# Two Fourier layers: written order on every engine, later statistics, scaling on GpSimd, and a second layer that takes x from the scaled images

## The chip, the cores and the metric

The kernel runs on one core of a Trainium2 chip. The metric is device time in microseconds of one execution. A core has TensorE (PE, with PEld for its weight loads), VectorE (DVE), ScalarE (ACT), GpSimd (POOL), and SyncE (SP), which here only issues DMAs. All data are 32-bit floats.

## The reference

The input is x of shape (2, 56, 128, 128): two images with 56 channels. Two layers of the same form are applied, each `x = x + block(groupnorm(x))`. The group norm takes groups of four of the last axis's 128 positions, over all of an image's channels and rows. Cut to what matters, the block is:

```python
def spectral_conv(x, w, b):                      # 16 + 16 by 16 modes are kept
    xf = jnp.fft.rfft2(x, norm='forward')
    top = jnp.einsum('bihw,iohw->bohw', xf[:, :, :M1, :M2], _c(w[0]))
    bot = jnp.einsum('bihw,iohw->bohw', xf[:, :, -M1:, :M2], _c(w[1]))
    ...
    return jnp.fft.irfft2(of, s=(H, W), norm='forward') + b[None, :, None, None]

xa = x.reshape(B * K, 1, H, W)                   # B = 2 images, K = 56 channels
xn = inorm(xa, g1, b1)
k, q, v = (fno_layer(xn, ...) for each)          # spectral_conv + 1x1 skip, 8 heads
scores = jnp.einsum('baks,bals->bakl', qh, kh) * scale
out = jnp.einsum('bakl,bals->baks', jax.nn.softmax(scores, axis=-1), vh)
out = fno_layer(out, Pw, Pb, Psw, Psb)
att = inorm(out + xa, gan, ban)
an = inorm(att, g2, b2)
h = fno_layer(an, M0w, ..., norm=True, act=True)  # act is the exact gelu
h = fno_layer(h, M1w, ..., norm=True, act=False)
y = inorm(h, gmo, bmo) + att
```

## The kernel before

An image lies in SBUF in `X2` with the channels on partitions, twice: rows of two kinds of eight on partitions 0 to 55 and 64 to 119. Two more partitions (56 and 120) hold a row of scales. Nearly all of the block is done on the 32 x 16 kept modes, in tiles of 448 columns; full images are touched only for the transform, for the gelu and for the end. A full image is handled in eight pieces ("units") of 1024 columns, numbered n = 2A + v.

For each layer L and image b the work is a set of Python generators. Each emits instructions and yields a number, its cost in microseconds as the author sees it:

- `turn` / `turned` transpose eight rows on PE (L361 in layer 0, L363 in layer 1), copy them on ACT (L366, L369) into the tile `P[b]` and take `bn_stats` on DVE (L371). `modes_chain` makes mean and scale from them (L459 to L468), scales the plane (L477 on ACT, L479 on DVE), transforms along one axis (L483), transposes on DVE (L488), and transforms along the other (L384).
- `gram` (L511), `gram_chain`, `scores` (L597, L578), `values` (L620), `softmax_chain`, `mix_chain`, `heads` (L691) and `norms_chain` do attention and the norms by way of small matrices. `scale_x` multiplies the whole image by the scales of its groups, in place, in eight DVE instructions of 120 x 1024 (L550), and then writes the scale rows with two DMAs.
- `gelu`: synthesis of each unit (L753), a matmul with the scaled image (`mixed`, L768), Gelu on ACT (L835), `bn_stats` on DVE (L837), transposing back (`turn_back`, L817, L818) and a transform (`forward`, L805, and a DVE copy, L810).
- `h_chain`: transposes on DVE (L851), small matrices, a chain of small DVE and ACT steps, the diagonals `dg` (L432), their spread by a matmul (L437), and `inverse` (L399, L404).
- `end`: synthesis (L753), `mixed` (L768), a sum on DVE (L943) and the residual x. In layer 0, and for image 0 of layer 1, POOL adds x from the ring `xr` of three buffers (L946), loaded from DRAM. Layer 0 writes image 0 to the DRAM tile `store` for this. For image 1 of layer 1, x is made again from the scaled image: `unscale` multiplies it on DVE, in place, by the inverse scales (L775), and `add_x` adds it by a matmul (L782). Layer 0 then calls `turned` for the next layer.
- `prepare` and `relay` make weight matrices of a layer (some 95 small POOL instructions; then PE L316, DVE L320, PE L327, ACT L331), and `build` / `build_m` expand them on POOL (L337, L345).

`_woven(lead, *bulks)` runs a lead chain and, after each of its yields, as many pieces of the bulks as their costs fill. `_with` steps a second generator once per piece. The Python order is thus one written order. It is not the order in which the engines run: the framework's scheduler orders the instructions of each engine by dependences and its own costs when the program ends. In `build`, `build_m` and `scale_x`, `tc.keep_in_program_order` binds single instructions.

PSUM is handed out as two `bank` tiles (2 KB per partition) and three `pair` tiles (4 KB). SBUF tiles with one name share one place, so that a new use waits for the readers of the old one.

## Time and profile before

| what | value |
|---|---|
| median of 3 runs | 551.45 us (550.92 to 551.50) |
| profiled execution | 547.76 us, span 546.0 us |
| PE busy | 458.8 us, 84% of the span |
| DVE busy | 318.6 us, 58% |
| ACT busy | 190.3 us, 35% |
| POOL busy | 158.5 us, 29% |
| HBM read, written | 21.02 MB, 11.01 MB |
| mean granted PE clock | 0.919 |

The span is the time from the first to the last recorded instruction, and the profiled execution is a single run with 1.76 us around that span. A line such as L768 names a line of the kernel printed above. In a group, "out<-in" are tile names, then the shape of output and input, then the busy time in us, the mean duration in ns, and the idle time just before with what ended it. In a stretch the columns are its length, then busy time and count of each engine, the granted PE clock, the share of the DMA engines that was busy, and GB/s.

### The profile page before, as it was taken

What the parts mean: (1) busy time and instruction counts of PE and PEld (TensorE: products, weight loads), DVE (VectorE), ACT (ScalarE), POOL (GpSimd) and SP (SyncE); (2) the same over time, 40 slices, a digit from 0 to 9 for tenths busy, and PEclk for the clock granted to TensorE, in tenths of its full rate; (3) what the DMA queues carried; (4) which work ended last, traced back from release to release, by engine and by line L of the source; (5) the groups of instructions that cost most, each with busy time, mean ns of one, the idle gap of its engine ahead of it and who ended that gap; (6) DMA issues with size and microseconds to landing.
All of it is one profiled execution on the core that took longest, in us unless ns stands there. A gap on an engine that the chain in (4) does not pass through costs nothing.

```text
span 546.0 us, 14842 instructions
## 1 busy us (share of the span) xinstructions
PE 458.8 (84%) x6696; PEld 315.0 (58%) x6696; DVE 318.6 (58%) x556; ACT 190.3 (35%) x242; POOL 158.5 (29%) x205
## 2 busy tenths in 40 slices
PE   2467999898699999989587799989599999986695
PEld 2325869686485566636443468778376556544431
DVE  1465352926735784777578562717715775766585
ACT  2443330524435436614223240344237356502000
POOL 2297509950000000044539924000000000055300
PEclk9998898989797998989679999999797998988698
DMA  8994001030100000016553320000000000027444
GB/s 181 232 196 73 4 2 46 4 89 2 20 2 2 1 2 1 1 35 212 175 136 100 98 78 6 3 4 4 2 3 1 1 2 1 1 56 236 149 129 141
DMA packets 13167, 33.24 MB, mean 61 GB/s; under 512 B 2080, under 2 KB 2848, under 8 KB 13088
## 3 DMA queue, kind: packets, MB, share of 16 engines
q1 hardware_dynamic: 12960, 32.23, 22.8%
q8 instruction: 52, 0.85, 0.7%
q10 hardware_dynamic: 144, 0.07, 0.1%
q14 instruction: 11, 0.09, 0.1%
HBM read 21.02 MB, written 11.01 MB: 59 GB/s over the span
## 4 chain that ended last, share of the span: by engine, by line
PE 53%; DVE 20%; POOL 7%; DMA 7%; ACT 6%; issue 5%; SPq 1%; DVEq 0%; POOLq 0%; ACTq 0%
PE pair L768 8%; PE pair L753 6%; PE pair L817 5%; POOL X L946 5%; PE pair L597 5%; PE bank L511 5%; PE bank L691 3%; DMA X<-x 3%; PE bank L805 3%; DMA xr<-x 3%; DVE WT L404 2%; DVE X L550 2%; PE bank L578 2%; PE bank L442 2%; PE bank L327 2%
## 5 line engine op out<-in xcount | busy, mean ns | idle before, releaser
L371 DVE BATCH_NORM_STATS2 stats<-P 128x6 f32<-128x448 f32 x64 | 36.1, 614 | 48.2 <-ACT P L366 32.3
L837 DVE BATCH_NORM_STATS2 stats<-P 128x6 f32<-128x512 f32 x64 | 40.7, 678 | 20.3 <-ACT P L835 20.3
L943 DVE SCALAR_TENSOR_TENSOR P<-P,hs,pair 128x1024 f32<-128x1024 f32 x32 | 40.1, 1270 | 12.7 <-PE pair L768 12.5
L835 ACT ACTIVATE P<-pair 128x1024 f32<-128x1024 f32 x32 | 32.6, 1025 | 32.4 <-PE pair L768 31.8
L946 POOL TENSOR_TENSOR X<-P,xr 128x1024 f32<-128x1024 f32 x16 | 37.5, 2355 | 19.4 <-DMA xr<-x 11.2
L393 POOL MEMSET WT<- 128x256 f32 x4 | 1.3, 313 | 139.4 <-PE bank L805 92.9
L817 PEld LDWEIGHTS pair<-C,P 120*128 120x128 f32 x256 | 29.0, 152 | 21.2 <-issue 8.5
L550 DVE TENSOR_TENSOR X<-X,gvr 120x1024 f32<-120x1024 f32 x32 | 40.3, 1303 | 0.0
L768 PE MATMUL pair<-X,Bs 57*64 57x512 f32 x256 | 40.2, 671 | 0.0
L768 PE MATMUL pair<-X,Be 57*64 57x512 f32 x256 | 38.6, 705 | 0.0
L817 PE MATMUL pair<-C,P 120*128 120x120 f32 x256 | 36.8, 291 | 0.5 <-DVE P L404 0.5
L511 PE MATMUL bank<-P 128*64 128x56 f32 (+1 forms) x1024 | 37.2, 238 | 0.0
L511 PEld LDWEIGHTS bank<-P 128*64 128x64 f32 (+1 forms) x1024 | 35.5, 152 | 2.1 <-issue 1.5
L597 PEld LDWEIGHTS pair<-xf,WU 64*64 64x64 f32 x1024 | 32.8, 135 | 5.3 <-issue 4.5
L597 PE MATMUL pair<-xf,WU 64*64 64x56 f32 x1024 | 35.9, 221 | 0.0
L818 ACT COPY WT<-pair 128x896 f32<-128x896 f32 x32 | 28.9, 906 | 14.0 <-PE pair L817 12.5
L753 PE MATMUL pair<-C,WT 32*128 32x128 f32 x512 | 24.1, 294 | 9.1 <-DVE WT L404 4.4
L753 PEld LDWEIGHTS pair<-C,WT 32*128 32x128 f32 x512 | 19.4, 189 | 20.5 <-issue 12.0
L369 ACT COPY P<-pair 128x896 f32<-128x896 f32 x16 | 14.5, 907 | 46.3 <-PE pair L363 46.3
L361 PE MATMUL pair<-C,X 56*128 56x56 f32 x256 | 16.7, 282 | 16.4 <-DMA X<-x 10.7
L363 PE MATMUL pair<-C,X 120*128 120x120 f32 x128 | 18.8, 297 | 13.4 <-POOL X L946 13.4
L363 PEld LDWEIGHTS pair<-C,X 120*128 120x128 f32 x128 | 14.9, 155 | 23.3 <-POOL X L946 20.0
(235 smaller groups left out, 850.0 us busy)
## 6 DMA issues: line engine op xcount, KB each, us to landing
X<-x SPq DMA_DIRECT2D x16, 448.0 KB
xr<-x SPq DMA_DIRECT2D x32, 224.0 KB
out<-P SPq DMA_DIRECT2D x32, 224.0 KB
store<-X SPq DMA_DIRECT2D x16, 224.0 KB
xr<-store SPq DMA_DIRECT2D x16, 224.0 KB
stage<-weights SPq DMA_DIRECT2D x2, 544.0 KB
C<-const_all SPq DMA_DIRECT2D x1, 621.0 KB
X<-x SPq DMA_DIRECT2D x2, 256.0 KB
```

The source lines that it names most:

```text
L363: T.transpose(p[:, s, N * e : N * e + 120], X2[:120, b, i, :], ident[:120, :120])
L371: V.bn_stats(stats[:, 2 * g + s, :], dst[:, 448 * s : 448 * s + 448])
L511: T.matmul(p[u : u + m, :K], lhsT=P[b][:, K * i : K * i + m], rhs=plane[b][:, i, :], start=(i < 2), stop=(i == N - 1), tile_position=(0, u ...
L550: tc.keep_in_program_order(V.tensor_tensor(v, v, _bc(st["gvr"][:120], 1, 8), ALU.mult))
L597: T.matmul(p[64 * e : 64 * e + 64, k, K * a : K * a + K], lhsT=WUv[64 * e : 64 * e + 64, t + k, a, :], rhs=xv[64 * e : 64 * e + 64, t + k, ...
L753: T.matmul(both[j // 2][:, j % 2, N * e : N * e + N], lhsT=Z[32 * j : 32 * j + 32, o : o + N], rhs=C["gw"][32 * j : 32 * j + 32, :], start ...
L768: T.matmul(p[64 * c : 64 * c + 64, r, :], lhsT=Bs[q, :], rhs=X2[q, b, s : s + 4, :].rearrange("p e w -> p (e w)"), start=False, stop=stop, ...
L817: T.transpose(p[:, r, N * e : N * e + 120], h3[:120, o : o + N], ident[:120, :120])
L835: S.activation(h3, both[v].rearrange("p r m -> p (r m)"), AF.Gelu)
L837: V.bn_stats(stats[:, 4 * A + 2 * v + r, :], h3[:, 512 * r : 512 * r + 512])
L943: V.scalar_tensor_tensor(h3, h3, st["hs"], both[v].rearrange("p r m -> p (r m)"), ALU.mult, ALU.add)
L946: G.tensor_tensor(dst, h3, xr[:, n % 3, :], ALU.add)
```

## The change

- **Order.** After the whole program is traced, `_in_order` adds a dependence, without a wait, from each instruction to the one before it on the same engine, for DVE, ACT, POOL, PE and SP. The engines' order is then the written one. The single `keep_in_program_order` calls go.
- **One unit late.** `turned` returns its statistics as a function, which `turn` and `end` call after the next piece; `gelu` defers the statistics and the copy of `forward` to after the next Gelu; `end` defers the sum (and what follows it) of a unit to after the matmuls of the next one.
- **Fillers.** `_woven` gets `spare`, a generator from which pieces are taken only if the bulks have run out. `scores` of image 1 and `gelu` of image 0 become such fillers, and the calls are rearranged. `scale_x` stands as a block behind the scores of its image. `prepare(1)` stands behind that of image 1. Relay of layer 1's weights moves to the end of image 0.
- **Scaling on POOL.** `scale_x` and `unscale` use POOL instead of DVE. `unscale` writes to the ring `xr` instead of in place.
- **x of the second layer.** Both images of layer 1 use `unscale` and `add_x`. The DRAM tile `store`, its 16 writes and its 16 reads go, and so does the POOL addition there.
- **Smaller edits.** In `modes_chain` the four scalings are written ahead, and transforms and transposes go by two in a pair (two DVE transposes of 896 columns for four of 448). `t` in `norms_chain` and `h_chain` moves from a bank to a pair. `mix_chain` and `heads` share one pair. The yielded costs are changed.

Core of the diff (renamings of queues and most changed costs are left out):

```diff
+def _in_order(tc, engines):
+    last = {}
+    for i in list(tc.nc.cur_bb.bb.instructions):
+        if i.engine in engines:
+            if i.engine in last:
+                info = mybir.DependencyInfo(mybir.DependencyClass.NoSync, mybir.DependencyReason.DATA)
+                tc.add_manual_dep(i, last[i.engine], info, reason="in order")
+            last[i.engine] = i.name
...
-def _woven(lead, *bulks):
+def _woven(lead, *bulks, spare=()):
...
             if cost is None:
+                cost = next(spare, None) if spare else None
+            if cost is None:
                 break
...
     def turn(b, stats):
+        before = None
         for g in range(8):
-            turned(b, g, 0, stats)
-            yield 0.9
+            count = turned(b, g, 0, stats)
+            if before:
+                before()
+            before = count
+            yield 1.1
+        before()
...
+        for j in range(0, 4, 2):
+            p = pair()
+            for k in range(2):
...
+                yield 0.6
+            V.transpose(
+                midv[:, :, 14 * j : 14 * j + 28].rearrange("p m (k i) -> p k i m", k=2),
+                p[:, :, :448].rearrange("p k (h i) -> p k i h", h=32),
+            )
...
     def scale_x(b, st):
         for s in range(0, 64, 8):
             v = X2[:120, b, s : s + 8, :]
-            tc.keep_in_program_order(V.tensor_tensor(v, v, _bc(st["gvr"][:120], 1, 8), ALU.mult))
+            (G.tensor_tensor(v, v, _bc(st["gvr"][:120], 1, 8), ALU.mult))
...
     def mix_chain(L, b, st):
+        st["pair"] = pair()
...
-        t = bank()[:, :448]
+        t = pair()[:, 0, :448]
...
     def unscale(b, A, v, by):
...
-        V.tensor_tensor(x8, x8, _bc(_bc(by[:120], 1, 4), 1, 2), ALU.mult)
+        to = xr[:120, (2 * A + v) % 3, :].rearrange("p (c s w) -> p c s w", c=2, s=4)
+        (G.tensor_tensor(to, x8, _bc(_bc(by[:120], 1, 4), 1, 2), ALU.mult))
...
                     S.activation(h3, both[v].rearrange("p r m -> p (r m)"), AF.Gelu)
-                    for r in range(2):
-                        V.bn_stats(stats[:, 4 * A + 2 * v + r, :], h3[:, 512 * r : 512 * r + 512])
-                    yield 0.9
+                    settle()
+                    after.append(lambda n=2 * A + v, h3=h3: count(n, h3))
+                    yield 1.1
...
+        def total(n, p):
+            h3 = P[b][:, 1024 * n : 1024 * n + 1024]
+            V.scalar_tensor_tensor(h3, h3, st["hs"], p.rearrange("p r m -> p (r m)"), ALU.mult, ALU.add)
+            if L == 0:
+                G.tensor_tensor(X2[:, b, 8 * n : 8 * n + 8, :].rearrange("p e w -> p (e w)"), h3, xr[:, n % 3, :], ALU.add)
+            else:
+                for c in range(2):
+                    Q.dma_start(
+                        out=far[b, c, :, n // 2, 2 * (n % 2) : 2 * (n % 2) + 2],
+                        in_=h3[64 * c : 64 * c + K].rearrange("p (r m) -> p r m", r=2),
+                    )
+            if L == 0:
+                ready(n + 2)
...
+        for A in range(4):
+            if before:
+                before()
+                before = None
             both = [pair(), pair()]
             synthesis(A, both, st["Z"])
             yield 1.0
             for v in range(2):
                 n = 2 * A + v
+                mixed(L, b, A, v, both[v], st["Be"], L == 0)
+                if L == 1:
+                    add_x(n, both[v])
+                    ready(n + 2)
+                if before:
+                    before()
+                before = lambda n=n, p=both[v]: total(n, p)
+                yield 2.1 if L == 1 else 1.1
+                if L == 0 and n > 2:
+                    counts.append(turned(b, n - 3, 1, stats))
+                    if len(counts) > 1:
+                        counts.pop(0)()
+                    yield 1.0
...
+        ux1, g0 = scores(L, 1, s1), gelu(L, 0, s0)
+        _run(_woven(gram_chain(L, 1, s1), scores(L, 0, s0)))
+        _run(scale_x(0, s0))
+        _run(_woven(softmax_chain(L, 0, s0), values(L, 0, s0), spare=ux1))
+        _run(_woven(mix_chain(L, 0, s0), heads(L, 0, s0), spare=ux1))
+        _run(_woven(norms_chain(L, 0, s0), ux1, values(L, 1, s1)))
+        _run(scale_x(1, s1))
         if L == 0:
             par, d, cpt, tcs = prepare(1)
             prs[1] = par, d
+        _run(_woven(softmax_chain(L, 1, s1), spare=g0))
+        _run(_woven(mix_chain(L, 1, s1), heads(L, 1, s1), spare=g0))
+        _run(_woven(norms_chain(L, 1, s1), g0))
         _run(_woven(h_chain(L, 0, s0), gelu(L, 1, s1)))
         stats = [new_stats(b) for b in range(B)] if L == 0 else [None, None]
+        more = relay(cpt, tcs, stage[:, :1024], [(0, 16), (16, 16), (32, 4)]) if L == 0 else iter(())
+        _run(_woven(h_chain(L, 1, s1), _with(end(L, 0, s0, stats[0]), more)))
...
+    _in_order(tc, [e.engine for e in (V, S, G, T, Q)])
```

In `ready(n)`, layer 0 loads unit n of x from DRAM into `xr`, and layer 1 calls `unscale` for it; two units are readied ahead of the loop.

## The prediction

> **What bounds the kernel now.** First the page: busy shares, then the slices.
>
> ```profile
> PE 458.8 (84%) x6696; PEld 315.0 (58%) x6696; DVE 318.6 (58%) x556; ACT 190.3 (35%) x242; POOL 158.5 (29%) x205
> PE   2467999898699999989587799989599999986695
> POOL 2297509950000000044539924000000000055300
> PEclk9998898989797998989679999999797998988698
> ```
>
> TensorE (PE) is the only engine near full. It has holes at the start and around slices 10, 19-23 and 36-38, and its clock drops beside most of them. POOL rests for long stretches. Second the stretches, cut where the work changes: columns are length, busy PE, PEld, DVE, ACT, POOL, clock, DMA.
>
> ```profile
> 0.00:51.90 51.90, 26.65 (x285) 17.79 (x285) 22.71 (x48) 18.87 (x22) 27.78 (x84) 1.00 0.83 179
> 51.90:94.60 42.70, 41.41 (x886) 35.91 (x885) 17.24 (x33) 10.34 (x17) 22.59 (x17) 0.88 0.06 17
> 94.60:158.40 63.80, 53.70 (x950) 44.25 (x948) 36.07 (x64) 23.18 (x31) 23.00 (x46) 0.92 0.12 25
> 158.40:233.70 75.30, 72.79 (x834) 46.00 (x832) 51.31 (x107) 40.53 (x49) 0.33 (x2) 0.93 0.01 2
> 233.70:275.80 42.10, 35.10 (x356) 22.37 (x358) 27.36 (x48) 11.04 (x16) 20.23 (x12) 0.81 0.51 153
> 275.80:316.80 41.00, 30.94 (x364) 16.26 (x364) 28.14 (x37) 12.31 (x14) 33.58 (x19) 0.95 0.42 109
> 316.80:342.00 25.20, 24.18 (x580) 18.91 (x576) 11.25 (x19) 5.93 (x10) 8.64 (x10) 1.00 0.12 21
> 342.00:408.00 66.00, 57.65 (x1136) 47.96 (x1137) 34.18 (x62) 24.56 (x32) 3.02 (x5) 0.95 0.04 3
> 408.00:479.00 71.00, 68.65 (x798) 41.80 (x800) 46.97 (x94) 39.70 (x46) 0.22 (x1) 0.93 0.01 1
> 479.00:514.80 35.80, 24.69 (x282) 14.91 (x278) 23.92 (x33) 3.89 (x8) 19.08 (x9) 0.81 0.52 159
> 514.80:546.00 31.20, 23.09 (x256) 8.78 (x256) 19.42 (x16) 0.00 (x0) 0.00 (x0) 0.90 0.41 129
> ```
>
> In order: start; gram, attention, gelu, end of image 0, end of image 1 (layer 0); the same five for layer 1. Gram and gelu are PE-bound. Attention loses 10.1 and 8.4 us, the first three ends 7.0, 10.1 and 11.1 us. Third the timeline, at two such holes.
>
> ```profile
> 139.85 0.86 PE L652 MATMUL bank<-C,P 56*64 56x56 f32 x10 [5.29 <-DVE Bs L450]
> ...
> 503.15 2.34 POOL L946 TENSOR_TENSOR P<-P,xr 128x1024 f32<-128x1024 f32 x1 [2.30 <-DVE f L881]
> ...
> 503.90 1.63 DVE L432 TENSOR_SCALAR dg<-C,f,sm 56x56 f32<-56x56 f32 x1
> 505.45 0.29 DVE L432 TENSOR_SCALAR dg<-C,c,r 56x56 f32<-56x56 f32 x1
> ```
>
> PE waits 5.3 us for the end of a chain of small DVE work, with nothing else ahead in its queue. And a 0.29 us DVE instruction takes 1.63 us while POOL runs a long one.
>
> **What the Trainium skill says.** "GPSIMD Engine Reference", Elementwise: a two-tensor add costs GpSimd 1.96 times VectorE. Here 2.355 us (L946) against 1.214 us (median of L550): agrees. "SBUF — State Buffer", Who interferes with whom: a GpSimd instruction that reads SBUF and a VectorE one with two SBUF inputs, or a scalar operation in the two-port mode, exclude each other for a whole instruction. The lines at 503 us agree. "TensorE: Matmul & The Clock Gate", What's actually happening: an idle window of about 3.4 us halves the clock. After the hole at 384 us the clock stands at 0.50 from 388 to 392 us: agrees. But it is 0.58 over 412 to 420 us with PE busy 7.78 of 8, so not every drop is bought by idleness. "PSUM — Partial Sum Buffer", Engine vs sequencer instructions: the other engines' queues are strict FIFO. Everything below on queues rests on that.
>
> **The change, part by part.** PE figures per image and layer are quarters of a group's busy time on the page or in the groups by shape (scores L597 35.9/4 and L578 17.6/4, values L620 and L629 5.8, synthesis plus mixing in an end 15.7, L363 a half: 9.4); they are estimates in so far as the clock varied under them.
>
> *Scaling moves to POOL.* Removed from DVE: 32 of L550 (40.3 us) and 8 of L775 (9.5 us). Added to POOL: 32 + 16 instructions. Their price is between the broadcast form of L337 (1.95 us) and L946 (2.355 us), 94 to 113 us; I take the upper. Eight L946 on P go (18.8 us). The eight for image 0 queue after four WT builds, two of L345, and the tables of `scores`. Their 19 us lie beside gram and scores work of image 1 and 0, and gelu needs them some 35 us later, so with their two row DMAs they cost nothing. The eight for image 1 start once POOL has copied `bm`, in the norms chain of image 0, and run beside it.
>
> *Behind them stands BT's memset of image 1*, which the matmul L671 waits for (before it ran at 117.27 us, ahead of need). In layer 0 `prepare(1)` is also written in between; its rows sum to about 20 us of POOL. From the `bm` copy POOL needs 8 x 2.35 + 20 = 39 us. PE has between `Pm` and L671: rest of scores 11.3, multiply, sums and spread 3.8, values 5.8, inverse 2.5, gelu units 6, L652, L664 and heads 4.2, waits about 2; together 35.6. **Stall 3.5 us in layer 0** (0 to 10); none in layer 1, where POOL has 19 us in front.
>
> *Norms chain of image 0 beside the scaling.* Six of its DVE instructions (three `dg`, the `syn` scaling, two one-row ones) can each wait for a POOL instruction, up to 2.35 us. Two segments, covered by PE work of 5 and 3.75 us against 2 to 3 us of bare chain: I take 4 us per layer (0 to 14).
>
> *Attention fillers.* Scores of image 1 now fill norms of image 0, and gelu of image 0 fills softmax of image 1; `t` moves to a pair, so L652 is no longer held by the bank that Bs releases. Idle recovered: 10.1 and 8.4, plus 2.8 and 2 us of slow clock in the rebound (about 4 to 6 us of work at half rate). New: the first Gelu waits behind Exp and a table load (1.28 us), and with three pairs the next synthesis waits for it: 2.2 us. Net layer 0: -12.9 + 3.5 + 4 + 2.2 = **-3.2**. Layer 1: -10.4 + 4 + 2.2 = **-4.2**.
>
> *Written order in gram.* Before, scores matmuls (L597 from 65.8 us) fill modes_chain of image 1; as written they come after gram of image 1. Gram's eight pieces are used up by the first pair of transposes, so the second doubled transpose (2 x 1.02 us and its handover, 2.4 us) is bare in both layers, and in layer 0 two relay groups wait for four DVE masks each (4 x 0.41, 2 us). Idle of 1.3 us there goes. **+5 and +2.** At the start, turn pieces that wait for loads stand in front of L463 (at 29.04 us before): **+2.5** (0 to 5); the loads end near 45 us either way.
>
> *Statistics and sums one unit late.* bn_stats (0.68 us) and STT (1.27 us) no longer stand in front of chain work while waiting for ACT or PE. In gelu, PE-bound, that is worth **-1.5** and **-1**.
>
> *Relay moves* from gelu to the end of image 0 in layer 0: 6.7 us of PE (L327 5.8, L316 0.9), with its DVE masks and ACT copies. Gelu -6.6. In the end stage PE work becomes 34 at full clock + 6.7, plus 3 of holes: 43.6 against 42.1, **+1.5; together -5.1**.
>
> *The DRAM detour goes.* 16 stores and 16 loads of 224 KB leave SP's queue. In layer 0 a load no longer waits behind a store that waits for POOL (L946 waited 11.2 us for DMA); the chain's late pieces are filled. End of image 1: PE 31 + 5 of waits for POOL's 19 + 8 us of sums and builds: 36 against 41, **-5**.
>
> *x from the scaled images.* Layer 1, image 0: 64 matmul instructions more, 8.7 us by L782's row. Full-clock work about 22 + 8.7 + 3 of holes = 33.5 against 35.8: **-2.3**. Image 1: POOL unscales ahead (8 x 2.35 = 19 us) instead of DVE between two PE steps; PE stays the bound at about 5.5 us per two units. The inverse scale is now computed at the start rather than in the hole before it: +2. The X waits of 4 us and 2 of slow clock shrink: **-2**.
>
> **Sum:** +2.5 + 5 - 3.2 - 1.5 - 5.1 - 5 + 2 - 4.2 - 1 - 2.3 - 2 = **-14.8 us** on a profiled execution of 547.76 us (span 546.0 and 1.76 around it). The median of the runs, 551.45, is 3.7 us higher for the same code, so I take the difference off the median: about **537 us**.
>
> **Rivals.** *POOL paces the chains, and it gets slower.* Place: attention, from `bm` of image 0 to L671. If each of the twelve exposed DVE instructions of the two layers waits a whole 2.35 us, 28 us instead of the 8 counted. If `prepare(1)` is stretched as the small L295 was beside DVE (1.29 against 0.32 us at worst, half of its entries), the stall in layer 0 is 13 instead of 3.5. That is up to +30: 567 us; half of it, **553 us**, already ends above the old time. It decides once new waits exceed the counted ones by 15 us. For it: the line at 503.90. Against it: during that time no 40 us of DVE scaling stand in the same queue, and most chain instructions read PSUM. Taken at three quarters: 559 us.
>
> *The ends don't shrink.* PE takes 8.7 us more and the loads were hidden anyway: end stages 0 instead of -5, -2.3 and -2, and relay unhidden +4: about **550 to 551 us**, no change. Against it: L946's waits for DMA.
>
> *More is recovered.* The written order closes gram's holes too (+7 becomes 0) and the exposed DVE waits don't show (8 becomes 0): **522 us**.
>
> *The order was the written one already.* Excluded: L597 at 65.8 us runs ahead of gram of image 1, which is written before it.
>
> **Numbers.** Forecast 525 to 545: 0.46; more recovered: 0.10; small gain, down to 1 us: 0.10; no change: 0.06; slower: 0.28, half of that above 560. Faster 0.66, same 0.06, slower 0.28 (0.2%, 1.1 us, is about what a measurement of this kernel can tell). The range, 521 to 562, leaves out about 0.08 below and 0.12 above.
>
> **What would show it.** Right: no PE hole over 3 us in attention; L597 after the second gram; in layer 1's ends no DMA into xr; about 5 us of PE waiting for POOL before L671 in layer 0. Wrong: L432 or other small DVE instructions over 1 us long in many places; PE waiting over 10 us for L667; clock near 0.8 still in the ends; the first transposes of image 1 holding back L463 by over 5 us.

## The result, and the profile after

The changed kernel takes 591.62 us (median of 4 runs, 586.91 to 600.87) against 551.18 us of the kernel before on the same chip: **1.071 times before, 95% interval 1.064 to 1.078**. Forecast was 537. The profiled execution of after took 593.02 us (span 591.2, mean granted clock 0.896), that of before 547.76 us (546.0, 0.919): 45.2 us more in the spans.

Times of one kernel spread by 1 to 3%, and the kernel before had medians of 550 to 559 us beside the runs below, so every run is given as a ratio to the runs of before that were measured together with it, and executions more than 1.5% above the fastest of their kernel are left out of the ratios. A profile shows one execution; differences of a few us between two profiles are read with that in mind.

The page of after, the lines that answer to the first fence of the prediction:

```profile
PE 469.2 (79%) x6762; PEld 319.3 (54%) x6762; DVE 295.9 (50%) x510; ACT 189.7 (32%) x242; POOL 243.5 (41%) x245
PE   3356868989489899879876777989489989859885
POOL 1391427945990000013448645963800000009274
PEclk9999595999789998967897998998887799879888
```

PE is busy 10 us longer than before, at a lower mean clock, yet its share of the longer span falls from 84 to 79%. POOL has gained 85 us of work and now fills slices 9 to 11 and 25 to 28 (counted from 0), where it rested; behind the start PE has its deepest holes in slices 10 and 28, inside those blocks, and the clock stands at 0.5 in slices 4 and 6.

The stretches of after, cut at the same events as the table of before (start, gram, attention, gelu, end of image 0, end of image 1, and the same for layer 1; columns as there):

```profile
0.00:66.50 66.50, 31.96 (x319) 22.04 (x319) 27.43 (x50) 21.44 (x23) 23.20 (x63) 0.94 0.64 140
66.50:108.50 42.00, 34.35 (x600) 29.27 (x599) 12.73 (x22) 6.44 (x12) 26.25 (x20) 0.77 0.05 15
108.50:171.80 63.30, 53.01 (x1045) 41.80 (x1042) 27.62 (x42) 23.79 (x30) 47.94 (x58) 0.92 0.12 26
171.80:251.20 79.40, 71.17 (x948) 45.70 (x944) 47.51 (x97) 40.63 (x50) 6.03 (x23) 0.96 0.01 2
251.20:310.00 58.80, 46.73 (x453) 30.72 (x449) 35.78 (x66) 11.62 (x19) 20.92 (x10) 0.83 0.24 67
310.00:350.70 40.70, 28.82 (x316) 16.60 (x316) 28.36 (x35) 12.00 (x13) 26.91 (x15) 0.92 0.21 58
350.70:374.00 23.30, 19.91 (x438) 14.46 (x438) 7.20 (x12) 5.28 (x7) 14.48 (x15) 0.93 0.01 2
374.00:440.50 66.50, 56.27 (x1103) 45.28 (x1106) 26.30 (x44) 23.82 (x31) 39.61 (x24) 0.90 0.04 4
440.50:523.70 83.20, 76.04 (x956) 48.21 (x948) 47.51 (x98) 40.87 (x50) 0.71 (x3) 0.90 0.01 2
523.70:557.00 33.30, 27.03 (x336) 14.34 (x336) 19.22 (x34) 3.78 (x8) 18.86 (x9) 0.85 0.26 79
557.00:591.20 34.20, 23.91 (x286) 10.92 (x278) 16.19 (x14) 0.00 (x0) 18.58 (x8) 0.90 0.47 140
```

The holes (length less busy PE) are what the forecast wanted closed. Attention keeps 10.3 us of them in layer 0 (10.1 before) and 10.2 in layer 1 (8.4 before), though its DVE work in layer 0 fell from 36.1 to 27.6 us. Gram of layer 0 had 1.3 and has 7.7. The end of image 0 in layer 0 had 7.0 and has 12.1. Only the end of image 0 in layer 1 closed some (11.1 to 6.3).

The timeline of after at slice 10: start, duration, engine, line, operation, and in brackets the idle time with its releaser.

```profile
139.54 18.47 POOL L575 TENSOR_TENSOR X<-X,gvr 120x1024 f32<-120x1024 f32 x8
...
147.37 10.97 DVE L453 TENSOR_SCALAR dg<-C,k,der 56x56 f32<-56x56 f32 x2
...
158.62 0.92 PE L458 MATMUL bank<-dg,ones 56*128 56x168 f32 x2 [7.82 <-DVE dg L453]
```

A DVE instruction that takes 0.29 us elsewhere runs from 147.37 until POOL's eight scalings are over (its longest single record is 10754 ns), and PE is idle for 7.82 us. The same happens at 416 to 427 us. I had priced such a wait at one POOL instruction, 2.35 us.

### The profile page after: what moved, and what is told of

The parts are those of the page before. It is cut to its first block, busy times and chain, and to the rows that moved or that the text cites. A ratio compares the mean times of both kernels' runs of the same rounds, so it can differ in the third digit from the quotient of the medians.

```text
span 591.2 us, 14943 instructions
## 1 busy us (share of the span) xinstructions
PE 469.2 (79%) x6762; PEld 319.3 (54%) x6762; DVE 295.9 (50%) x510; ACT 189.7 (32%) x242; POOL 243.5 (41%) x245
## 4 chain that ended last, share of the span: by engine, by line
PE 53%; DVE 16%; ACT 7%; issue 6%; POOL 3%; ACTq 0%; DVEq 0%; POOLq 0%
PE pair L794 8%; PE pair L779 5%; PE pair L622 5%; PE bank L536 4%; DVE dg L453 4%; PE pair L851 4%; PE pair L717 3%; PE pair L645 3%; PE bank L339 3%; PE bank L463 2%; PE bank L405 2%; ACT WT L852 2%; PE pair L808 2%; PE bank L839 2%; PE bank L603 2%
## 5 line engine op out<-in xcount | busy, mean ns | idle before, releaser
L575 POOL TENSOR_TENSOR X<-X,gvr 120x1024 f32<-120x1024 f32 x32 | 74.1, 2348 | 0.2
L802 POOL TENSOR_TENSOR xr<-X,gvr 120x1024 f32<-120x1024 f32 x16 | 37.2, 2364 | 87.1 <-DVE gvr L958 72.1
L373 PE MATMUL pair<-C,X 56*128 56x56 f32 x256 | 18.6, 314 | 31.0 <-DMA X<-x 25.3
L851 PE MATMUL pair<-C,P 120*128 120x120 f32 x256 | 34.6, 284 | 2.1 <-DVE WT L425 1.1
L373 PEld LDWEIGHTS pair<-C,X 56*128 56x128 f32 x256 | 15.8, 217 | 36.0 <-DMA X<-x 19.0
L622 PE MATMUL pair<-xf,WU 64*64 64x56 f32 x1024 | 33.1, 219 | 0.0
L622 PEld LDWEIGHTS pair<-xf,WU 64*64 64x64 f32 x1024 | 31.1, 135 | 2.4 <-issue 1.7
L779 PE MATMUL pair<-C,WT 32*128 32x128 f32 x512 | 25.7, 338 | 5.1 <-DVE P L963 2.0
L779 PEld LDWEIGHTS pair<-C,WT 32*128 32x128 f32 x512 | 21.5, 233 | 12.9 <-issue 5.7
L779 PE MATMUL pair<-C,P 32*128 32x128 f32 x512 | 23.4, 297 | 6.1 <-ACT P L869 4.1
```

The lines of the kernel that those rows point to most:

```text
L575: (G.tensor_tensor(v, v, _bc(st["gvr"][:120], 1, 8), ALU.mult))
L622: T.matmul(p[64 * e : 64 * e + 64, k, K * a : K * a + K], lhsT=WUv[64 * e : 64 * e + 64, t + k, a, :], rhs=xv[64 * e : 64 * e + 64, t + k, ...
L779: T.matmul(both[j // 2][:, j % 2, N * e : N * e + N], lhsT=Z[32 * j : 32 * j + 32, o : o + N], rhs=C["gw"][32 * j : 32 * j + 32, :], start ...
L802: (G.tensor_tensor(to, x8, _bc(_bc(by[:120], 1, 4), 1, 2), ALU.mult))
L851: T.transpose(p[:, r, N * e : N * e + 120], h3[:120, o : o + N], ident[:120, :120])
```

## The experiments

The theory after reading these traces had two parts: small DVE instructions are held for POOL's whole run (about 9 us per layer), and the rest is lost at single places of the written order. The rival was that the moved work itself, not the order, costs the time.

**1. DVE beside runs of POOL, by itself.** Behind the end of the kernel before:

```
 for k in range(n):
     G.tensor_tensor(x[k], x[k], gvr row, mult)     # 2.3 us each, back to back
     if k == 0: one 56x56 DVE instruction that reads x[0]
```

> The kernel before with eight trials added behind its end. In each, GpSimd multiplies a run of tiles of image 0's x by the scale row (120x1024 from and to SBUF, back to back), and one small VectorE instruction of 56x56 reads what the first of the run wrote, so that it may start when the second starts. Runs: 8, 4 and 2 tiles beside a tensor_scalar; 8 tiles beside a tensor_scalar with a short pause after the fourth (GpSimd waits for a ScalarE copy there); 8 half-size tiles beside a tensor_scalar; 8 tiles beside scalar_tensor_tensor, tensor_tensor and tensor_copy. Theory A (the VectorE instruction is held until the run ends): tensor_scalar takes (n - 1) x 2.35 us: 16.5, 7.1 and 2.4 us; with the pause about 7.1 us, as it gets in there; beside half-size tiles about 7 x 1.2 = 8.4 us; scalar_tensor_tensor and tensor_tensor under 0.6 us; tensor_copy like tensor_scalar. Theory B (held for the instruction that runs, as I predicted): every one of them ends within 2.4 us of its start, whatever the length of the run.

DVE's timeline of that run, the eight trials in order:

```profile
551.33 2.31 DVE L1020 TENSOR_SCALAR stage<-X,eps 56x56 f32<-56x56 f32 x1 [2.68 <-POOL X L1016]
569.87 6.90 DVE L1020 TENSOR_SCALAR stage<-X,eps 56x56 f32<-56x56 f32 x1 [16.23 <-POOL X L1016]
579.38 2.31 DVE L1020 TENSOR_SCALAR stage<-X,eps 56x56 f32<-56x56 f32 x1 [2.62 <-POOL X L1016]
584.30 6.90 DVE L1020 TENSOR_SCALAR stage<-X,eps 56x56 f32<-56x56 f32 x1 [2.62 <-POOL X L1016]
602.25 8.55 DVE L1020 TENSOR_SCALAR stage<-X,eps 56x56 f32<-56x56 f32 x1 [11.04 <-POOL X L1016]
613.41 16.11 DVE L1021 SCALAR_TENSOR_TENSOR stage<-X,eps 56x56 f32<-56x56 f32 x1 [2.61 <-POOL X L1016]
632.13 16.11 DVE L1022 TENSOR_TENSOR stage<-X,eps 56x56 f32<-56x56 f32 x1 [2.61 <-POOL X L1016]
650.86 16.09 DVE L1023 COPY stage<-X 56x56 f32<-56x56 f32 x1 [2.61 <-POOL X L1016]
```

Runs of 4 and 2 hold it 6.90 and 2.31 us, three times and once a tile; a pause of POOL (fourth line, a run of 8 cut in the middle) lets it in; half-size tiles hold it for the whole run too. So theory A in the main, with three misses: scalar_tensor_tensor and tensor_tensor are held as well, and the very first trial, beside a run of 8, got in at the next boundary. Why that one did is not settled, and it is not the only one. In the trace of after_pe_only (part 6) the inverse row got in between two scalings of a longer run:

```profile
357.43 4.69 POOL L575 TENSOR_TENSOR X<-X,gvr 120x1024 f32<-120x1024 f32 x2
...
357.90 1.98 DVE L955 TENSOR_SCALAR gvr<-C,gv 128x128 f32<-128x128 f32 x1
```

And in the trace of after a tensor_scalar of 128x56 (L760, 1.03 us) came in where POOL's L283 ended and L284 followed. So a hold often lasts for the run, but not always.

**2. Which instructions.** Nine more trials beside runs of four (the last: eight).

> The kernel before with nine more trials behind its end, made like those of the first run of that kind: GpSimd multiplies four tiles back to back (eight in the last trial), and one VectorE or ScalarE instruction may start when the second begins. In order: tensor_scalar of 56x56, of 56x1, of 56x8; tensor_tensor of 56x56 with one operand in PSUM; tensor_scalar of 56x56 into PSUM; bn_stats of 56x56; a ScalarE copy of 56x56; tensor_scalar of 56x56 where each tile was just touched by ScalarE, so that each GpSimd instruction has a wait of its own (already met); tensor_scalar of 56x56 beside eight tiles. Theory A (what is held is an instruction that moves enough from SBUF to SBUF; the kernel's own 56x1 and 56x3 instructions ran in 0.2 us inside such a run): 6.9 us in the first, 0.2 in the second, 6.9 in the third, 0.2 to 0.4 with an operand in PSUM, 6.9 for bn_stats, 0.3 on ScalarE, 2.3 in the one with waits (the first trial of the first run ended at the next boundary, and its tiles came fresh from other engines), 16.1 in the last. Theory B (it is a matter of when the instruction comes, not of what it is): 2.3 and 6.9 or 16.1 mixed over all VectorE forms alike, PSUM or not.

Seven of the nine, from the timeline of that run:

```profile
556.18 6.90 DVE L1028 TENSOR_SCALAR stage<-X,eps 56x56 f32<-56x56 f32 x1 [2.97 <-POOL X L1022]
...
565.70 0.26 DVE L1026 TENSOR_SCALAR stage<-X,eps 56x1 f32<-56x1 f32 x1 [2.62 <-POOL X L1022]
...
575.05 6.88 DVE L1027 TENSOR_SCALAR stage<-X,eps 56x8 f32<-56x8 f32 x1 [9.09 <-POOL X L1022]
...
584.54 0.21 DVE L1029 TENSOR_TENSOR stage<-bank,X 56x56 f32<-56x56 f32 x1 [2.61 <-POOL X L1022]
...
593.89 0.33 DVE L1030 TENSOR_SCALAR bank<-X,eps 56x56 f32<-56x56 f32 x1 [6.48 <-POOL X L1022]
...
603.25 0.21 DVE L1031 BATCH_NORM_STATS2 stage<-X 56x6 f32<-56x56 f32 x1 [8.78 <-POOL X L1022]
...
612.60 0.34 ACT L1032 ACTIVATE stage<-X,eps 56x56 f32<-56x56 f32 x1 [91.89 <-POOL X L1022]
```

One operand or the result in PSUM sets a DVE instruction free, and so does one element per partition; eight elements are enough to be held. bn_stats (expected to be held) and ScalarE are free. The trial in which POOL's instructions had met waits of their own was held too (6.90, where 2.3 was expected), the last took 16.09. Each form was tried once or twice.

The Trainium skill, "SBUF — State Buffer", Who interferes with whom, sorts the forms in the same way (copy and tensor_scalar can exclude GpSimd, under conditions on their operands, and so do instructions with two inputs in SBUF), and these runs agree for the forms tried. But it lets whoever came first keep the ports "for the whole instruction"; here DVE waited over up to seven instructions of POOL. The measurement decides.

**3. The held instruction in another form.**

```
-V.tensor_scalar(dg[:, j, :], ident[:K, :K], u, v, mult, mult)
+V.scalar_tensor_tensor(dg[:, j, :], ident[:K, :K], u, v.to_broadcast([K, K]), mult, mult)
```

> The kernel after with one instruction form changed: the rows of the norms and of the h chain (rows_of, L453) are made with scalar_tensor_tensor in place of tensor_scalar, same queue, same place. Theory A (held until a run of GpSimd instructions ends): TensorE's two idle stretches of 7.8 us before the first spread go, and the slow clock behind each; 15 to 20 us less, 573 to 578 by the profiled 593. Theory B (held for one instruction, the 10.75 us were something else): at most 4 us less, 587 to 592.

1.065 times before (1.053 to 1.077): the same as after. The instruction still took 10.77 us, as the trials say it must, so this run doesn't test the price of the hold. It does show something else: with every queue in the same order its span is 7.2 us shorter than that of after, and nearly all of it lies ahead of the end of Gram (the matmul L565 before rr of image 0 at 99.0 against 106.0 us). The last pieces of x landed at 43.9 instead of 49.4 us; other runs whose start has the same written order lie between. So far does the landing of x move one execution.

**4. Without the written order**, and with TensorE left out of it.

```
-    _in_order(tc, [e.engine for e in (V, S, G, T, Q)])            # after_sched
+    _in_order(tc, [e.engine for e in (V, S, G, Q)])               # after_free_pe
```

> The kernel after without the written order (the call of _in_order is left out): the scheduler orders all five queues, and nothing holds GpSimd's bulk in program order either; the scaling on GpSimd, the x of the second layer from the scaled images and the delayed statistics stay. Theory A (the written order is the larger part of the loss: the start, the Gram stage, the ends): 30 to 45 us less, 548 to 563. Theory B (the moved work is the loss: the scaling on GpSimd with what it holds up, and the scaled x): at most 15 us less, 578 or more.

> The kernel after with TensorE left out of the written order: VectorE, ScalarE, GpSimd and SyncE keep it, the scheduler orders TensorE's instructions. Theory A (heads of TensorE's own queue wait while other matmuls are ready: the turn pieces at the start, the waits for the inverse scale and for the woven-in relay): 15 to 25 us less, 568 to 578. Theory B (the waits come from VectorE's queue, where the awaited instruction stands behind others, so that TensorE has nothing else ready): within 8 us of after, 585 to 600.

Without it: **0.9997 times before (0.997 to 1.003)**. The whole loss goes with this written order; POOL's scaling, the scaled x and the late statistics add up to nothing under the scheduler. With TensorE alone freed: 1.035 (1.024 to 1.046), half of the loss, theory A.

**5. Repairs of single places, order kept.**

```
after_scale1: (V if b else G).tensor_tensor(v, v, gvr row, mult)      in scale_x
after_start:  _run(_woven(modes_chain(0, 0, ...), islice(t1, 2)))     t1 = turn(1, ...)
              _run(_woven(relay(...), islice(t1, 4)));  rest of t1 into gram(0)
after_ends:   relay chained to norms_chain(L, 1), L955-L958 ahead of h_chain(L, 0)
after_three:  all of these
```

> The kernel after with the eight scalings of image 1's x (scale_x) back on VectorE, at the same place of the written order; image 0's stay on GpSimd. Theory A (the norms of image 0 lose some 9 us in each layer because their rows on VectorE are held until GpSimd's run of eight scalings ends): the 10.75 us of L453 become 0.3, the rows are spread 9 us earlier in each layer, and the time falls by 12 to 20 us, to 572 to 580. Theory B (TensorE's queue or image 1's chain decides in that stretch, and 8 x 1.24 us on VectorE ahead of its softmax cost the gain again): at most 5 us less, 587 or more.

> The kernel after with the turn pieces of image 1 written elsewhere: two behind image 0's statistics, four beside the relay of layer 0's coefficients, the last two among the first pieces of image 0's Gram stage (before: six of the eight in front of image 0's width transforms). Theory A (the transforms stand behind turn pieces that wait for x): the first L509 starts 3 to 4 us earlier, the Gram stage 5 to 7, and the time falls by 5 to 10 us, to 581 to 587. Theory B (the landing of x sets the start, and image 1's own chain comes later by what image 0's gains): within 3 us of after, 588 to 595.

> The kernel after with two things written earlier: the relay of layer 1's coefficients stands between the norms of image 1 and the Gelu stage again, as in the kernel before, in place of the end of image 0; and the inverse scale row of layer 1 (L955 to L958) is made for both images ahead of the h chain of image 0, in place of the head of each end. Theory A (both stand in queues where what they wait for comes late): the 4.4 us wait of L339, the slow clock behind it and the 5.8 and 3.9 us waits of L957 go, while the Gelu stage takes back some 4 us; 10 to 18 us less, 573 to 581. Theory B (the relay costs the Gelu stage as much as the end gains, and something else is late at the end in place of the inverse row): at most 5 us less, 586 or more.

> The three edits together (image 1's scaling on VectorE, the turn pieces at the start, the relay and the inverse row): the written order is kept. Theory A (the losses are separate and add up): 30 to 45 us less than after, 547 to 562, about the kernel before. Theory B (they overlap, the written order costs by its whole length and not at three places): 570 or more.

| kernel | times before | interval |
|---|---|---|
| after_scale1 | 1.063 | 1.052 to 1.073 |
| after_start | 1.061 | 1.050 to 1.072 |
| after_ends | 1.075 | 1.064 to 1.085 |
| after_three | 1.061 | 1.051 to 1.072 |

None of the intervals is clear of that of after (1.064 to 1.078). Scale1, ends and three came out as their theories B; the interval of after_start covers both of its theories. My theory of separate places fell. after_scale1 shows how a gain is spent again. DVE's timeline of it:

```profile
157.90 0.60 DVE L771 TENSOR_TENSOR D<-D,bank 128x448 f32<-128x448 f32 x1
158.43 9.15 DVE L575 TENSOR_TENSOR X<-X,gvr 120x1024 f32<-120x1024 f32 x8
167.51 0.38 DVE L663 TENSOR_TENSOR bank<-bank,rr 128x224 f32<-128x224 f32 x1
```

L453 takes at most 0.36 us now, and the norms of image 0 end at 157.9 instead of 169.6 us. But the eight scalings stand next in the queue, and image 1's softmax (L663) starts at 167.5 instead of 170.1: the 11.7 us are gone but for 2.6, and 1.2 of these stood already ahead of rr of image 0. In after_ends the two edits can be told apart by layer: layer 1, with the early inverse row, takes 274.0 us instead of 281.1; layer 0, with the relay back beside gelu, starts layer 1 at 315.1 instead of 310.1. By these two traces the relay costs 5 us more beside gelu than in the end of image 0: image 1's h chain begins 16.5 us later, since the gelu units of image 0 are used up and the relay stands bare, and the end then takes 46.6 instead of 58.1 us (42.1 before).

**6. Which queue.** The call of `_in_order` with other lists:

> The kernel after with the written order on TensorE alone; VectorE, ScalarE, GpSimd and SyncE are ordered by the scheduler. With TensorE alone freed the loss fell from some 38 to some 20 us, with all freed to none. Theory A (TensorE's written order makes its 20 us by itself, and the other queues theirs): 568 to 578. Theory B (only the two together are harmful, as each head that waits is covered when the other side may move): 552 to 562. Theory C (TensorE's order is the whole loss): 585 or more.

> The kernel after with VectorE alone left out of the written order (TensorE, ScalarE, GpSimd and SyncE keep it). Theory A (VectorE's written order puts image 1's softmax behind all of image 0's norms, 170.1 us in the trace of after against 145.3 where VectorE was free, and the transposes and counts ahead of what TensorE waits for): 1.02 to 1.045 times before. Theory B (VectorE only hands on what GpSimd's run holds up, its order is harmless): 1.06 or more. Theory C (VectorE is the whole of it): under 1.02.

> The kernel after with GpSimd alone left out of the written order. Where GpSimd was free (the written order on TensorE alone), its scaling of image 1 lay under the heads of image 0, ahead of the norms, and L453 took 0.3 us. Theory A (the place of the run costs some 9 us in each layer at the norms, and as much again at image 1's softmax, which stands behind them on VectorE; no 10 us of scaling are put on VectorE for it, as they were in the run with image 1's scaling there): 1.025 to 1.045 times before. Theory B (as with the scaling of image 1 on VectorE, the written order takes the gain back within the stage): 1.055 or more.

> The kernel after with VectorE and GpSimd left out of the written order; TensorE, ScalarE and SyncE keep it. With the written order on TensorE alone the ratio was 1.016. Theory A (the loss beside TensorE's own lies in these two queues): 1.01 to 1.025 times before. Theory B (ScalarE's or SyncE's order has a share): 1.03 or more.

All of them together, with the start of image 1's softmax (L663) in layer 0 by each trace (before: 133.7 us):

| order written for | times before | interval | L663 of image 1, us | from rr of image 0 (L569), us |
|---|---|---|---|---|
| no queue (after_sched) | 0.9997 | 0.997 to 1.003 | 140.9 | 41.1 |
| PE | 1.016 | 1.003 to 1.029 | 145.3 | 43.9 |
| PE, ACT, SP | 1.029 | 1.022 to 1.036 | 148.3 | 43.9 |
| PE, ACT, SP, POOL | 1.040 | 1.031 to 1.049 | 154.8 | 51.6 |
| PE, ACT, SP, DVE | 1.044 | 1.033 to 1.055 | 158.0 | 52.7 |
| DVE, ACT, POOL, SP | 1.035 | 1.024 to 1.046 | 158.2 | 57.6 |
| all five (after) | 1.071 | 1.064 to 1.078 | 170.1 | 63.2 |

The last column leaves out the start, in which the landing of x differs from trace to trace; before has 40.7 there. The trace of after_sched is of an execution of 556.2 us, 4.3 us above the median of its kernel.

No queue carries the loss. PE's order alone costs 1.6 points (theory B of its run), the other four 3.5, all together 7.1. That is 2.0 more than the sum, just beyond what the intervals can tell (about 1.8). Freeing DVE or POOL alone came out as theory A, and freeing both, 1.029, between its two theories. Under the scheduler, too, the order of each queue is set before the kernel runs, but it is set with the other queues in view. So the table fits queues that hand waits to each other: where the scheduler places one queue, it fills the hole that the written ones leave. That another written order, the scheduler's own for one, would lose as well isn't shown. Where PE alone is fixed, the timelines of POOL and DVE show what the two others do with their freedom:

```profile
110.03 9.28 POOL L575 TENSOR_TENSOR X<-X,gvr 120x1024 f32<-120x1024 f32 x4
```

```profile
141.85 0.52 DVE L453 TENSOR_SCALAR dg<-C,k,der 56x56 f32<-56x56 f32 x2
142.30 0.30 DVE L453 TENSOR_SCALAR dg<-C,k,sm 56x56 f32<-56x56 f32 x1
145.32 0.40 DVE L663 TENSOR_TENSOR bank<-bank,rr 128x224 f32<-128x224 f32 x1 [2.73 <-PE bank L603]
```

The scaling is over at 119.3 us, before the norms begin, so L453 isn't held, and DVE takes image 1's softmax while image 0's norms wait for PE. In after_free_pool the hold is gone too (0.30 us at most); from rr of image 0 in layer 1 (its matmul L565 stands at 373.4 us in both traces) the rows are spread at 418.2 instead of 427.6 us. That puts the price of the hold at 9.4 us in layer 1; in layer 0, counted from rr too, it is 7.9 us.

**7. One regrouping, order kept.** Softmax, values, mix and heads of image 1 among the units of image 0's norms, as before groups them:

```
-_run(_woven(norms_chain(L, 0, s0), ux1, values(L, 1, s1)))
+_run(_woven(norms_chain(L, 0, s0), ux1, _woven(softmax_chain(L, 1, s1), values(L, 1, s1)),
+            _woven(mix_chain(L, 1, s1), heads(L, 1, s1))))
```

> The kernel after, written order kept on all five queues, with image 1's softmax, values, mix and heads written among the units of image 0's norms again, as the kernel before groups them, in place of behind them (the Gelu units of image 0 then stand beside image 1's norms alone). Theory A (image 1's softmax on VectorE behind image 0's norms is a main loss; the units of TensorE that it frees fill the norms): image 1's attention ends 8 to 12 us earlier in each layer, 1.03 to 1.05 times before. Theory B (the order as such is the loss, and any one regrouping is paid for elsewhere): 1.055 or more.

1.095 (1.084 to 1.105), slower than after: theory B, and worse. The softmax starts 5.6 us earlier (164.5), but the first Gelu, with its table load, comes at 186.2 instead of 171.8 us. The gelu units that had filled PE in softmax and mix are now written behind them. A grouping that served the scheduler lost as a written order.

**8. Parts of the change under the scheduler.**

```
after_sched_dve:  after_sched, scale_x on VectorE, in program order
before_scaled_x:  the kernel before; layer 1 takes x from unscale into xr (GpSimd) and add_x (TensorE),
                  no store; L955-L958 ahead of h_chain(L, 0)
sched_kept:       after_sched; builds, scale_x of image 0, unscale and the additions of end
                  under tc.keep_in_program_order
sched_kept_early: the same, L955-L958 ahead of h_chain(L, 0)
```

> The kernel after without the written order and with all scaling of x back on VectorE, kept in program order there as in the kernel before. Beside the run without the written order (551.9 us) it shows what the scaling on GpSimd is worth once the scheduler places it. Theory A (GpSimd's runs hold VectorE in the softmax and norms stages, some 4 to 7 us in each of four places, which outweighs VectorE's freed 40 us): 535 to 546. Theory B (VectorE's freed time and the held instructions cancel): 548 to 556.

> The kernel before, with the scheduler's order, and one part of the change alone: x of the second layer comes from the scaled images (no store, no loads in layer 1; GpSimd writes x times the inverse row to xr, TensorE adds it for both images, and the inverse rows are made ahead of the h chain of image 0). Theory A (the ends of layer 1 are the part of the change that pays: from the norms of image 1 to the end of the run the scheduled kernel after took 105.9 us by its trace, before 123.6): 10 to 18 us less than before, 533 to 542. Theory B (the ends gain at most the GpSimd additions and the 48 transfers, which were hidden, while TensorE has 32 matmuls more of 0.27 us): 547 to 554.

> The kernel after without the written order, and with GpSimd's bulk kept in program order among itself (the building of the mode matrices, image 0's scaling, the additions of the ends and the inverse scaling; image 1's scaling stays free). In the run without the written order the scheduler put three scalings of layer 1 (L575, 321.8 to 328.7 us) ahead of the last addition of layer 0's end (L965), and TensorE waited 8.84 us for it. Theory A (that inversion costs what its wait says): 6 to 9 us less than without the written order, 0.983 to 0.99 times before. Theory B (the Gram stage of layer 1 waits for its builds or for image 1's statistics then): within 0.995 and 1.003.

> The same with the inverse rows of layer 1 made ahead of the h chain of image 0. In the written order this edit gave layer 1 some 7 us by the trace (the run with the ends changed: 274.0 us from layer 1's first statistics to the end, against 281.1). Theory A (the first L957 waits under the scheduler too, as it stands in the program behind the h chain of image 1): another 3 to 6 us less, 0.973 to 0.983 times before. Theory B (the scheduler had covered the wait): the same as its neighbour within 0.3%.

after_sched_dve gave 553.6 to 572.3 us (before: 556.9 median), too spread for a verdict; it does not show that VectorE is the better place. **before_scaled_x: 0.9915 (0.987 to 0.996)**, faster than both kernels, and nearer to theory B in size. Its trace is 4.0 us shorter than before's: layer 1 starts 4.3 us earlier (there are no stores among layer 0's loads any more, and POOL's waits for these loads, 11.2 us before, are gone from the list of its long waits), and the last end, from image 1's rows on, takes 34.5 instead of 40.2 us, but image 0's h chain in layer 1 falls back in between.

sched_kept: 0.9945 (0.991 to 0.998), also faster than before, but theory A asked for 0.983 to 0.99. It removes the wait that the timeline of after_sched shows:

```profile
321.82 6.95 POOL L575 TENSOR_TENSOR X<-X,gvr 120x1024 f32<-120x1024 f32 x3
328.72 2.34 POOL L965 TENSOR_TENSOR X<-P,xr 128x1024 f32<-128x1024 f32 x1
...
331.12 1.86 PE L375 MATMUL pair<-C,X 120*128 120x120 f32 x8 [8.84 <-POOL X L965]
```

and pays for it at the next place, by the timeline of sched_kept (its lines behind 575 are two higher, so L957 there is L955 of after):

```profile
350.29 16.23 POOL L575 TENSOR_TENSOR X<-X,gvr 120x1024 f32<-120x1024 f32 x7
...
366.48 0.93 POOL L596 TENSOR_TENSOR P<-C,der 56x448 f32<-56x448 f32 x1
...
367.44 4.63 POOL L575 TENSOR_TENSOR X<-X,gvr 120x1024 f32<-120x1024 f32 x2
...
359.11 13.29 DVE L957 TENSOR_SCALAR gvr<-C,gv 128x128 f32<-128x128 f32 x1
...
372.07 0.33 DVE L696 COPY BT<-bank 56x56 f32<-56x56 f32 x1
...
372.48 0.69 PE L699 MATMUL bank<-BT,C 56*128 56x64 f32 x2 [7.22 <-DVE BT L696]
```

The scheduler drops the inverse row, which nobody needs yet and which goes from SBUF to SBUF, into POOL's run. It is held for 13.29 us, until POOL's last scaling ends at 372.07, and BT, which PE waits for, stands behind it. sched_kept_early writes the row ahead of image 0's h chain, but the scheduler, which isn't bound to that place, puts it into the same run (L942 there):

```profile
363.12 13.30 DVE L942 TENSOR_SCALAR gvr<-C,gv 128x128 f32<-128x128 f32 x1
```

The ratio was 0.9973 (0.994 to 1.0005), the same as its neighbour: theory B. So what this hold costs was not tested; a version with the row bound to a place behind the run, or made from PSUM, wasn't tried.

## Why the prediction was wrong

The delay against before at events that both traces have, beside the forecast's running sum at the same event (layer 0, then layer 1):

| up to | forecast | measured |
|---|---|---|
| heads of image 0 (L729) | +7.5 | +18.6 |
| rows of image 0's norms | +11.5 | +27.6 |
| rows of image 1's norms | +4.3 | +29.1 |
| h chain of image 0 begins (relay moved out) | -3.8 | +16.7 |
| first statistics of layer 1 | -2.3 | +32.5 |
| rr of image 0, layer 1 | -5.3 | +34.8 |
| rows of image 1's norms | -9.5 | +52.0 |
| h chain of image 0 begins | -10.5 | +43.3 |
| end | -14.8 | +45.2 |

Forecast and measurement part by 60 us in all: 11.1 up to the heads of image 0, 9.4 in attention and gelu of layer 0, 14.3 in the end of image 0, 5.3 in the end of image 1 and the Gram of layer 1, 13.7 in attention and gelu of layer 1, 6.2 in its ends.

**What failed first is the step "Written order in gram", and under it a premise of all steps: that the written order leaves the existing overlap and adds fillers.** I priced the order where I saw it move something, +9.5 us (start +2.5, gram +5 and +2). after_sched shows that it costs 7.1 points, some 39 us, and that the rest, which I priced at -24.3 with the fillers that the order places, brings nothing without it. In time it begins with the start and Gram: measured is 18.6 us by the heads of image 0 against 7.5. The start grew, with six turn pieces that wait for loads in front of the transforms, and the 9 us of scores that had filled Gram's chains were left for later; Gram's clock stood at 0.77. Some 7 us of this are the luck of the loads: in after_dg, where x landed near the 45 us that I had assumed, the delay is 11.7 us.

**"Attention fillers: idle recovered, -12.9 and -10.4" failed.** The holes in attention stayed at 10.3 and 10.2 us. The fillers were there, but DVE, ACT and POOL were in the written order as well, and L663 of image 1 moved from 133.7 to 170.1 us (from 40.7 to 63.2 behind rr of image 0). The table by queue supports this: freeing PE, DVE or POOL alone takes 2.7 to 3.6 points off.

**"Norms chain beside the scaling, 4 us per layer" was right in its mechanism and wrong in size**: 7.9 us in layer 0 and 9.4 in layer 1. The price that I took, one POOL instruction, is the term that was mis-sized; here the hold lasted for the rest of the run. The alternatives were counted over six instructions with a wait each, where in fact the first one held takes it all. The rival "POOL paces the chains" had the right sign and place, but not the mechanism: at the norms of image 0 the delay grows by 9.0 us in each layer, 18 of the 45 us before anything is won back, and 2.7 points of the 7.1 go where POOL's place is freed. (Its half-way time, given as 553 us, is 551 to 552 by its own terms.)

**"BT's memset, stall 3.5 us" did not show**: L693 ran at 177.71 us, L697 at 180.95, and PE didn't wait for POOL there. The chain ahead of it was late by more.

**"Relay moves: together -5.1" came out right in its sum by luck; both of its terms were wrong.** Moved back beside gelu (after_ends) the relay makes layer 1 start 5.0 us later, but gelu grows by 16.5 us, where I had 6.6, and the end of image 0 shrinks by 11.5, where I had charged 1.5. That charge is what failed: the end took 58.1 us where I had 43.6. In it L339 stands bare for 4.43 us (the trace names only "issue" as the cause; by the timeline the masks L332 that it reads were queued on DVE behind the h chain's transposes and ended 0.1 us before it), and its 16 matmuls then take 3.57 us at a clock of 0.50 (1.93 us for 16 alike at 1.00 at the start of after_dg). Without the relay the end is still 4.5 us longer than before.

**"The inverse scale is computed at the start, +2" was too small:** PE waits 5.79 and 3.9 us for L955, queued behind the h chain's transposes; made early, layer 1 gained 7.1 us (after_ends). The rest of "x from the scaled images" holds its sign: it is the one part that was run by itself, and it makes the kernel faster (before_scaled_x, with the row made early), by 0.85%, which is 4.7 of 551 us. The terms for the late statistics were not run alone.

**Held:** L597 of image 0 came after the second Gram, and no DMA into xr was left in layer 1. Of the signs that I had named for being wrong, the clock near 0.8 in the ends came true (0.83 and 0.85, in the ends of image 0), and the transform's first matmul (L463 before, L484 now) was held back by 5.4 us, though by 2.2 in after_dg. Small DVE instructions over 1 us came at four places only, but two of them took 10.7 us.

## What to carry to other kernels

Writing the order of all queues by hand gives up what the scheduler does for each queue in view of the others. Here that was the whole loss. Cost it by naming, for every queue, what stands behind each wait, and test it queue by queue; here repairs of single places were spent again one stage later. Moving bulk work to GpSimd is not free for VectorE: before a back-to-back run, ask which small SBUF-to-SBUF instructions of VectorE fall into it, and keep those that others wait for out of it (freeing POOL's place did that here), or try a PSUM operand or a break in the run, which worked in the trials and were not tried in the kernel. A part that pays (here the scaled x) may hide in a bundle that loses; run it alone under the old order.

## What the hardware showed that I had not expected

A VectorE instruction of 0.2 to 0.3 us from SBUF to SBUF, started beside the second of four or eight GpSimd instructions running back to back, took 6.90 and 16.1 us, until the last of them ended, and 10.75 and 13.29 us inside the kernels. A GpSimd pause of 0.29 us let it in. With one operand or the result in PSUM, or with one element per partition, it took 0.2 to 0.3 us in the same place. Three cases remain unexplained, which ended at the next boundary of the run: one trial of 2.31 us beside a run of eight, L955 with 1.98 us and L760 with 1.03 us.
